# Fixing TensorE's order in the edge stage of a four-layer graph network

## The chip, the cores and the metric

The kernel runs on one core of a Trainium2 chip. The metric is the time of one execution on the device, in microseconds (us); lower is better. The times below are medians of several executions, and a profile is one further execution, with a time of its own.

## The reference

A graph of 3125 nodes and 103125 directed edges (50000 edges in both directions, and a loop at every node), sorted by destination, goes through four layers with a residual and a layer norm around each:

```python
x = _layernorm(x + _L0_gnn_ref(x, src, dst, edge_weight, L0_gnn_weight, L0_gnn_b))   # weighted sum over edges, relu
x = _layernorm(x + _L1_gnn_ref(x, edge_index, ...))                                  # attention, four heads
x = _layernorm(x + _L2_gnn_ref(x, L2_gnn_Wq, ..., edge_index))                       # attention, one head
x = _layernorm(x + _L3_gnn_ref(x, edge_index, ...))                                  # two mean aggregations
```

Layer 0 matters here: with `xw = x @ weight`, every edge adds its weight times `xw[dst]` to its source node's row; then bias and relu.

## The kernel before

The nodes are padded to 3200, 25 blocks of 128. Rather than gather and scatter edge by edge, the kernel turns the edge list into two dense 3200 x 3200 matrices in DRAM: counts of edges (`f_ctd`, bf16, used by layers 1 to 3) and sums of edge weights (`wd`, float32, used by layer 0). The stage that does it is the edge stage, inside `fast_path` (line 506 on).

**Batches and groups.** Five destination nodes make a window; there are 640 windows, in 40 batches of 16 (loop at line 852). A window has 256 slots for edges, in two halves of 128, one edge to a partition. For each slot the kernel makes two one-hot rows: `ohd` (the source's place in its block, 128 wide) and `ohc` (destination in the window and source block, 125 of 128 used). `make(b)` (line 811) does it for a whole batch on VectorE: `ohd` and `ohc` by comparing keys with a ramp (line 824), then `wod`, the one-hots of the source scaled by the weight in three bf16 parts (line 833). The second half of the third part is scaled by ScalarE, a window at a time, in `more(k)` (line 842). `make(b + 1)` is called as batch b begins.

Within a batch, four groups of four windows follow each other. A group is eight counting matmuls (line 864: out `cp`) and 24 weighted matmuls (line 872: out `wp`), each into a PSUM bank; ScalarE copies `cp` into `cs` (line 877) and `wp` into `ws` (line 883). After a batch, `ws` is stored to `wd` in two DMAs (line 885), and after every second batch `cs` is stored to `f_ctd` (line 888). All of these DMAs are issued by SyncE (SP), whose queue is taken in order.

**Keys.** The keys of a batch come from `keys_of(g)` (line 652), once for eight batches: three columns of a gathered table are copied out (VectorE and ScalarE), TensorE transposes them in six steps (lines 672 to 674), and VectorE and ScalarE make from these the bf16 pairs that `make` reads. For groups 2 to 4 the source calls `keys_of` in `make` at batches 10, 18 and 26 (one batch ahead, so while batches 9, 17 and 25 are traced).

**Layer 0 within the edge stage.** As soon as 128 further rows of `wd` are written, `add0` (line 784) loads them (the columns of the first 20 blocks, in two DMAs of 640 KB into tiles `cw`, line 790) and multiplies them by a block of `xw` in 20 float32 matmuls (line 794) that add to five PSUM banks, `acc0`. There are 25 such blocks of rows; those whose rows are not ready when the 40th batch ends follow after it. `end0` (line 799) then takes relu, residual and layer norm. The last five column blocks (`left`) are summed afterwards, in 25 more loads, while layer 1 begins.

**Buffers.** One-hots `ohd`, `ohc` have two buffers each (line 564), `wod` six, two batches' worth (line 565); PSUM tiles `cp` and `wp` share three banks (line 567); `cw` has three (line 806), so a load can run at most three tiles ahead of the products that read it; `cs` and `ws` have two (line 807).

**What sets the order.** The kernel is written for a tracing layer: the source says what depends on what, and a scheduler places each engine's instructions, taking those that it expects to be ready, by priority in the order of the source. It also adds all waits. So the source's order and the order on an engine are not the same: in the program before, the 20 matmuls of one `add0` stand together as one burst, in the midst of some group, and the bursts lie about one and a half batches apart. Once built, the order on each engine is fixed.

Of the kernel before, what the change touches and what calls it, by code (L numbers as in the profile page):

```python
# [8 lines left out]
BF16 = mybir.dt.bfloat16  # L9
# [6 lines left out]
P = 128  # L16
# [476 lines left out]
BW = 16  # L493
KW = WN * NB
NBT = NW // BW
Z0 = 20
# [9 lines left out]
def fast_path(  # L506
# [4 lines left out]
    nc = tc.nc  # L511
# [46 lines left out]
    xw = cst.tile([P, NB, P], F32, name="f_xw")  # L558
# [4 lines left out]
    kp = front.enter_context(tc.tile_pool(name="kp", bufs=2))  # L563
# [85 lines left out]
        )  # L649
        egs.append(eg)  # L650

    def keys_of(g):

        eg = egs[g]
        kd2 = kp.tile([P, P // BW, 2, BW, 2], BF16, name="kd2")
        kc2 = kp.tile([P, P // BW, 2, BW, 2], BF16, name="kc2")
        w2 = [kp.tile([P, P // BW, 2, BW, 2], BF16, name=f"w2_{s}") for s in range(3)]
        kic = ep.tile([P, EW], F32, name="kic", bufs=2)
        nc.vector.tensor_scalar(
            kic.rearrange("p (a k) -> p a k", k=16), eg[:, :, 0, :], thr[:, g : g + 1], None, OP.subtract  # L660
        )

        nc.vector.memset(kic[:, EW - 1 : EW], -1.0)
        kid = ep.tile([P, EW], F32, name="kid", bufs=2)
        nc.vector.tensor_copy(kid.rearrange("p (a k) -> p a k", k=16), eg[:, :, 1, :])
        wei = ep.tile([P, EW], F32, name="wei", bufs=2)
        nc.scalar.copy(wei.rearrange("p (a k) -> p a k", k=16), eg[:, :, 2, :])
        t0 = cps.tile([P, 4, P], F32, name="t0", tag="cw")
        t1 = cps.tile([P, 2, P], F32, name="t1", tag="cw")
        for h in range(2):  # L670
            a = slice(h * P, (h + 1) * P)
            nc.tensor.transpose(t0[:, h, :], kid[:, a], ident)
            nc.tensor.transpose(t0[:, 2 + h, :], kic[:, a], ident)
            nc.tensor.transpose(t1[:, h, :], wei[:, a], ident)

        def each(i, h):
            return i[:, h, :].rearrange("p (b w) -> p b w", w=BW)

        def pairs(i, h):
            return each(i, h)[:, :, :, None].to_broadcast([P, P // BW, BW, 2])  # L680

        wt = ep.tile([P, 2, P], F32, name="wt", bufs=2)
        wu = kp.tile([P, 2, P], F32, name="wu")
        for h in range(2):
            copy(kd2[:, :, h, :, :], pairs(t0, h))
            copy(kc2[:, :, h, :, :], pairs(t0[:, 2:, :], h))
            nc.scalar.copy(w2[0][:, :, h, :, :], pairs(t1, h))
        for s, (i, o) in enumerate(((t1, wt), (wt, wu))):
            for h in range(2):
                nc.vector.tensor_tensor(each(o, h), each(i, h), w2[s][:, :, h, :, 0], OP.subtract)  # L690
                nc.scalar.copy(w2[s + 1][:, :, h, :, :], pairs(o, h))
        return kd2, kc2, w2, wu

    keys = {0: keys_of(0), 1: keys_of(1)}


    l0_wt = load("f_l0_wt", l0_w, [P, P])
# [82 lines left out]
    def bias0(acc, n):  # L780
        for j in range(n):
            nc.tensor.matmul(acc[:, j, :], ones, l0_br, start=(j == 0), stop=False, skip_group_check=True)

    def add0(pool, i, accs, blocks):

        b0, n = blocks
        for h in range(0, n, 10):
            m = min(10, n - h)
            cw = pool.tile([P, min(10, n), P], F32, name="cw")[:, 0:m]
            nc.sync.dma_start(  # L790
                cw.rearrange("p c d -> p (c d)"), wd[i * P : (i + 1) * P, (b0 + h) * P : (b0 + h + m) * P]
            )
            for j in range(h, h + m):
                nc.tensor.matmul(  # L794
                    accs[j // 4][:, j % 4, :], cw[:, j - h, :], xw[:, i, :], start=False,
                    stop=(i == NB - 1 and (j % 4 == 3 or j == n - 1)), skip_group_check=True,
                )

    def end0(acc, b0, n):
        t = lp0.tile([P, 4, P], F32, name="r0")  # L800
# [5 lines left out]
    zp = front.enter_context(tc.tile_pool(name="f_zp", bufs=3))  # L806
# [3 lines left out]

    def make(b):

        if b % 8 == 2 and 8 < b < NBT - 8:
            keys[b // 8 + 1] = keys_of(b // 8 + 1)
        kd2, kc2, w2, w3 = keys[b // 8]
        ohd = op_.tile([P, 2 * BW, P], BF16, name="ohd")
        ohc = op_.tile([P, 2 * BW, P], BF16, name="ohc")

        def twos(k):
            k = k[:, b % 8, :, :, :].rearrange("p q w t -> p (q w) t")  # L820
            return k[:, :, None, :].to_broadcast([P, 2 * BW, P // 2, 2])

        for o, k in ((ohd, kd2), (ohc, kc2)):
            nc.vector.tensor_tensor(
                o.rearrange("p w (a t) -> p w a t", t=2), twos(k),
                ramp.rearrange("p (a t) -> p a t", t=2)[:, None, :, :].to_broadcast([P, 2 * BW, P // 2, 2]),
                OP.is_equal,
            )
        wod = []
        for s in range(3):  # L830
            f = of_.tile([P, 2 * BW, P], BF16, name="wod")
            n = 2 * BW if s < 2 else BW
            nc.vector.tensor_tensor(  # L833
                f[:, 0:n].rearrange("p w (a t) -> p w a t", t=2), ohd[:, 0:n].rearrange("p w (a t) -> p w a t", t=2),
                twos(w2[s])[:, 0:n], OP.mult,
            )
            wod.append(f)

        def more(k):
            for w in range(k, k + 4):  # L840
                at = (b % 8) * BW + w
                nc.scalar.activation(wod[2][:, BW + w, :], ohd[:, BW + w, :], AF.Copy, scale=w3[:, 1, at : at + 1])  # L842

        return ohd, ohc, wod, more

    cs = None
    acc0 = None
    done = 0
    cur = make(0)
    for k in range(0, BW, 4):  # L850
        cur[3](k)
    for b in range(NBT):
        ohd, ohc, wod, _ = cur
        cur = make(b + 1) if b + 1 < NBT else None
        if b % SB == 0:
            cs = sp.tile([P, NB, SB * BW * WN], BF16, name="cs")
        ws = sp.tile([P, BW, P], F32, name="ws")
        for k in range(0, BW, 4):
            cp = cps.tile([P, 4, P], F32, name="cp", tag="cw")
            wp = cps.tile([P, 4, P], F32, name="wp", tag="cw")  # L860
            for j in range(4):
                for q in range(2):
                    w = q * BW + k + j
                    nc.tensor.matmul(  # L864
                        cp[:, j, 0:KW], ohd[:, w, :], ohc[:, w, 0:KW], start=(j == 0 and q == 0), stop=(j == 3 and q == 1),
                        skip_group_check=True,
                    )
            for j in range(4):
                for q in range(2):
                    w = q * BW + k + j  # L870
                    for s in range(3):
                        nc.tensor.matmul(  # L872
                            wp[:, j, :], ohc[:, w, :], wod[s][:, w, :], start=(j == 0 and q == 0 and s == 0),
                            stop=(j == 3 and q == 1 and s == 2), skip_group_check=True,
                        )
            i0 = (b % SB) * BW * WN + k * WN
            nc.scalar.copy(  # L877
                cs[:, :, i0 : i0 + 4 * WN].rearrange("p c (w i) -> p c w i", i=WN),
                cp[:, :, 0:KW].rearrange("p w (i c) -> p c w i", c=NB),
            )  # L880
            if cur:
                cur[3](k)
            nc.scalar.copy(ws[:, k : k + 4, :], wp)  # L883
        for a, e in ((0, 112), (112, KW)):
            nc.sync.dma_start(wv_[b * BW : (b + 1) * BW, a:e, :].rearrange("w k d -> k w d"), ws[a:e, :, :])
        if b % SB == SB - 1:
            i0 = (b - SB + 1) * BW * WN
            nc.sync.dma_start(ctd[:, :, i0 : i0 + SB * BW * WN].rearrange("c d i -> d c i"), cs)
        if b < 2:
            for blocks in GB[4 * b : 4 * b + 4]:  # L890
                xw_of(*blocks)
        if b == 2:
            products_of_weights()
            acc0 = [zps.tile([P, 4, P], F32, name=f"acc{k}", tag=f"acc{k}") for k in range(Z0 // 4)]
            for a in acc0:
                bias0(a, 4)
        while acc0 and (done + 1) * P <= (b - 1) * BW * WN:
            add0(zp, done, acc0, (0, Z0))
            done += 1
    for i in range(done, NB):  # L900
        add0(zp, i, acc0, (0, Z0))
    front.close()
# [431 lines left out]
    with ExitStack() as st:  # L1334
# [79 lines left out]
        for x_, (q, c) in enumerate(items):  # L1414
# [6 lines left out]
            if q == 0 and NB - 4 <= c < NB - 1:  # L1421
                a = split + (c - NB + 4) * 512
# [6 lines left out]
            elif c == NB - 1:  # L1429
# [5 lines left out]
                for k0 in range(0, n, 3):  # L1435
# [5 lines left out]
                    for j in range(m):  # L1441
                        b = i0 + k0 + j
# [177 lines left out]
```

## Time and profile before

| | |
|---|---|
| median of 3 runs | 1538.35 us (1538.09 to 1540.38) |
| the profiled execution | 1536.56 us, span 1534.5 us |
| granted TensorE clock | 0.979 of full speed on average |
| TensorE, VectorE, ScalarE busy | 1400.5, 981.0, 923.4 us |
| first and last weighted matmul of the edge stage | 40.6 and 468.8 us after the span's start |
| last product into `acc0` | 497.9 us |

The span runs from the first to the last instruction; the time of the execution is 2.06 us longer. PE is TensorE's matmul, PEld its weight load, DVE is VectorE, ACT ScalarE, SP SyncE. A row of the timeline gives start and length of a run of equal instructions, and in brackets the idle time of the engine before it with what ended it. A matmul's end is modelled, so consecutive matmuls overlap in the records, and the distance from start to start is what one costs in a stream. A float32 product shows as two records.

### The profile page before, as it was taken

The numbers are of one execution on the slowest core, as the hardware profiler recorded it, in microseconds if no ns is written. First come the engines' busy times: TensorE is split into PE (matmuls) and PEld (weight loads), VectorE is DVE, ScalarE is ACT, GpSimd is POOL, SyncE is SP. The second block draws the span as 40 slices with busy tenths as digits, with TensorE's granted clock in tenths as the row PEclk, the third lists the DMA queues.
The fourth block names the chain that finished last, engine by engine and source line by source line (L and its number), as shares of the span: only waits on it lengthen the run. The fifth ranks groups of instructions, "written<-read, shape, count | busy, mean of one in ns | idle before, by whom it ended". The sixth has DMA issues, their size and how long they took to land.

```text
span 1534.5 us, 35155 instructions
## 1 busy us (share of the span) xinstructions
PE 1400.5 (91%) x14871; PEld 1223.6 (80%) x14871; DVE 981.0 (64%) x1574; ACT 923.4 (60%) x1880; POOL 122.5 (8%) x136
## 2 busy tenths in 40 slices
PE   4899999999997978899989989899999989999995
PEld 3898999998997867899979889577777764458995
DVE  4999899989991389778878887544464360012005
ACT  2988778888882489878778676544474340023006
POOL 1000000000000023203311320300000000000000
PEclk9999999999999999999999999999999999999998
DMA  6387787878877623444434333332222226513551
GB/s 192 91 220 207 203 234 206 235 202 223 214 214 232 222 85 101 143 118 125 132 115 134 114 87 95 106 94 68 67 72 73 82 105 238 193 44 129 195 195 45
DMA packets 210368, 224.39 MB, mean 146 GB/s; under 512 B 72892, under 2 KB 184007, under 8 KB 209945
## 3 DMA queue, kind: packets, MB, share of 16 engines
q1 hardware_dynamic: 206344, 217.74, 48.4%
q10 hardware_dynamic: 3457, 2.35, 0.6%
q8 instruction: 118, 1.93, 0.5%
q0 software_dynamic: 400, 1.97, 0.4%
q14 instruction: 49, 0.40, 0.1%
HBM read 157.67 MB, written 64.36 MB: 145 GB/s over the span
## 4 chain that ended last, share of the span: by engine, by line
PE 40%; DVE 5%; ACT 2%; issue 1%; POOL 1%; DMA 1%; DVEq 0%; ACTq 0%; SPq 0%; POOLq 0%
PE acc L1381 9%; PE s L1373 8%; PE acc L1476 7%; PE acc L1549 6%; PE acc L1241 4%; PE acc L1236 2%; DVE cm L1226 1%; DVE nz L1260 1%; PE tr L1513 1%; PE acc L1513 1%; DMA ct<-f_ctd 1%; ACT fm L1225 1%; DVE cm L1219 0%; PE tr L1505 0%; PE acc L1505 0%
## 5 line engine op out<-in xcount | busy, mean ns | idle before, releaser
L1241 PE MATMUL acc<-vp,cm 128*128 128x198 bf16 x2500 | 344.7, 252 | 6.6 <-DVE cm L1226 4.1
L1225 ACT ACTIVATE fm<-adr,bas 128x896 bf16<-128x896 f32 (+1 forms) x320 | 286.5, 952 | 68.0 <-DVE cm L1226 63.1
L1236 PE MATMUL acc<-vp,ct 128*128 128x204 bf16 x1250 | 315.2, 256 | 10.0 <-DVE vp L1144 5.6
L1241 PEld LDWEIGHTS <-cm 128*128 128x128 bf16 x2500 | 236.0, 98 | 26.5 <-issue 10.6
L872 PE MATMUL wp<-wod,ohc 128*128 128x128 bf16 x3840 | 244.0, 219 | 8.8 <-ACT cs L877 6.6
L872 PEld LDWEIGHTS <-ohc 128*128 128x128 bf16 x3840 | 224.0, 98 | 9.8 <-issue 9.4
L833 DVE TENSOR_TENSOR wod<-ohd,w 128x4096 bf16<-128x4096 bf16 (+1 forms) x120 | 225.0, 1931 | 0.6 <-PE wp L872 0.6
L1226 DVE TENSOR_TENSOR cm<-fm,ct 128x896 bf16<-128x896 bf16 (+1 forms) x320 | 198.1, 649 | 36.1 <-PE acc L1241 14.1
L842 ACT ACTIVATE wod<-ohd,wu 128x128 bf16<-128x128 bf16 x640 | 197.0, 400 | 0.0
L1377 DVE TENSOR_TENSOR e<-e,ct 128x416 f32<-128x416 f32 (+1 forms) x175 | 110.4, 636 | 108.2 <-ACT e L1376 102.6
L1376 ACT ACTIVATE e<-s,f_nm 128x416 f32<-128x416 f32 (+1 forms) x175 | 111.5, 642 | 99.4 <-PE s L1373 94.1
L1381 PEld LDWEIGHTS acc<-self__8127,e 128*128 128x128 f32 x1250 | 148.4, 193 | 21.5 <-issue 19.7
L1373 PE MATMUL s<-yT,f_xT 128*128 128x416 f32 (+1 forms) x350 | 145.8, 552 | 4.6 <-ACT rt L1356 4.0
L1381 PE MATMUL acc<-self__8127,e 128*128 128x129 f32 x1250 | 148.7, 276 | 0.6 <-DVE e L1377 0.6
L794 PE MATMUL acc<-f_xw,cw 128*128 128x128 f32 x1000 | 118.4, 278 | 7.4 <-DMA cw<-wd 7.4
L1236 PEld LDWEIGHTS <-ct 128*128 128x128 bf16 x1250 | 122.4, 98 | 2.5 <-issue 1.5
L883 ACT COPY ws<-wp 128x512 f32<-128x512 f32 x160 | 93.6, 585 | 49.8 <-PE wp L872 48.2
L794 PEld LDWEIGHTS acc<-f_xw,cw 128*128 128x128 f32 x1000 | 115.0, 194 | 7.6 <-DMA cw<-wd 7.6
L864 PE MATMUL cp<-ohc,ohd 128*128 128x125 bf16 x1280 | 96.7, 218 | 21.1 <-ACT ws L883 17.9
L1373 PEld LDWEIGHTS s<-yT,f_xT 128*128 128x128 f32 x350 | 62.2, 191 | 57.7 <-issue 40.6
L1476 PE MATMUL acc<-ct,ip 128*128 128x512 bf16 (+1 forms) x525 | 104.9, 360 | 1.4 <-DMA ct<-f_ctd 1.4
L1549 PE MATMUL acc<-ip,ct 128*128 128x128 bf16 x1875 | 105.2, 219 | 0.0
(277 smaller groups left out, 1482.7 us busy)
## 6 DMA issues: line engine op xcount, KB each, us to landing
ct<-f_ctd SPq DMA_DIRECT2D x50, 800.0 KB
wd<-ws SPq DMA_DIRECT2D x40, 896.0 KB
ct<-f_ctd SPq DMA_DIRECT2D x150, 224.0 KB
cw<-wd SPq DMA_DIRECT2D x50, 640.0 KB
f_ctd<-cs SPq DMA_DIRECT2D x20, 1000.0 KB
ct<-f_ctd SPq DMA_DIRECT2D x25, 416.0 KB
ct<-f_ctd SPq DMA_DIRECT2D x25, 384.0 KB
cw<-wd SPq DMA_DIRECT2D x25, 320.0 KB
```

The costliest lines, as they stand in the source:

```text
L794: nc.tensor.matmul(accs[j // 4][:, j % 4, :], cw[:, j - h, :], xw[:, i, :], start=False, stop=(i == NB - 1 and (j % 4 == 3 or j == n - 1)) ...
L833: nc.vector.tensor_tensor(f[:, 0:n].rearrange("p w (a t) -> p w a t", t=2), ohd[:, 0:n].rearrange("p w (a t) -> p w a t", t=2), twos(w2[s] ...
L842: nc.scalar.activation(wod[2][:, BW + w, :], ohd[:, BW + w, :], AF.Copy, scale=w3[:, 1, at : at + 1])
L872: nc.tensor.matmul(wp[:, j, :], ohc[:, w, :], wod[s][:, w, :], start=(j == 0 and q == 0 and s == 0), stop=(j == 3 and q == 1 and s == 2), ...
L1225: nc.scalar.activation(f[:, : n * P], at, AF.Relu, bias=bas[:, c, h : h + 1], scale=UP)
L1226: nc.vector.tensor_tensor(m[:, : n * P], f[:, : n * P], ct[:, : n * P], OP.min)
L1236: nc.tensor.matmul(out_(F1, PW), ct[:, k * P : (k + 1) * P], vp[:, c, hp : hp + 2, :, 2 * F1 : V1], start=(c == 0), stop=False, skip_group ...
L1241: nc.tensor.matmul(out_(0, 2 * F1)[:, j], ms[j][:, k * P : (k + 1) * P], vp[:, c, hp + j, :, 0 : 2 * F1], start=False, stop=(c == NB - 1 a ...
L1373: nc.tensor.matmul(s[:, :m], xT[:, c * P : (c + 1) * P], yT[:, i0 * P + a : i0 * P + a + m], start=True, stop=True)
L1381: nc.tensor.matmul(acc[k // 3][:, (k % 3) * (P + 1) : (k % 3 + 1) * (P + 1)], es[q, c][:, k * P : (k + 1) * P], vo[:, c, 0 : P + 1], start ...
L1476: nc.tensor.matmul(acc[k][:, :n], ips[b // 4][:, b % 4, s, :], ct[:, c : c + n], start=(b == 0 and s == 0), stop=(b == NB - 1 and s == 2),)
L1549: nc.tensor.matmul(acc[g][:, j, :], ct[:, (b0 + j) * P : (b0 + j + 1) * P], ups[b // 4][:, b % 4, s, :], start=(b == 0 and s == 0 and j == ...
```

## The change

Three things are changed, all in the edge stage. First, `add0` is divided: `adds0` issues the loads and returns the 20 matmuls as a list of functions; the loop puts them on a list, `todo`, and takes four from it behind each group. Second, after batch 2 (counted from 0) a context is entered in which the scheduler keeps the order of the source on TensorE alone; it is left when the last batch and the rest of `todo` are traced. The other engines are scheduled as before. Third, `keys_of` is divided: `columns_of` copies the columns out, called in `make` at batches 9, 17 and 25, and the transposes and all behind them are called at batches 11, 19 and 27.

```diff
-    def keys_of(g):
+    def columns_of(g):
         eg = egs[g]
...
         nc.scalar.copy(wei.rearrange("p (a k) -> p a k", k=16), eg[:, :, 2, :])
+        return kid, kic, wei
+
+    def keys_of(kid, kic, wei):
...
-    keys = {0: keys_of(0), 1: keys_of(1)}
+    keys = {g: keys_of(*columns_of(g)) for g in range(2)}
...
-    def add0(pool, i, accs, blocks):
+    def adds0(pool, i, accs, blocks):
         b0, n = blocks
+        todo = []
...
             for j in range(h, h + m):
-                nc.tensor.matmul(
-                    accs[j // 4][:, j % 4, :], cw[:, j - h, :], xw[:, i, :], start=False,
+                todo.append(lambda j=j, a=cw[:, j - h, :]: nc.tensor.matmul(
+                    accs[j // 4][:, j % 4, :], a, xw[:, i, :], start=False,
                     stop=(i == NB - 1 and (j % 4 == 3 or j == n - 1)), skip_group_check=True,
-                )
+                ))
+        return todo
+
+    def add0(*args):
+        for f in adds0(*args):
+            f()
...
     def make(b):
-        if b % 8 == 2 and 8 < b < NBT - 8:
-            keys[b // 8 + 1] = keys_of(b // 8 + 1)
+        if b % 8 == 1 and 8 < b < NBT - 8:
+            keys[b // 8 + 1] = columns_of(b // 8 + 1)
+        if b % 8 == 3 and 8 < b < NBT - 8:
+            keys[b // 8 + 1] = keys_of(*keys[b // 8 + 1])
...
             nc.scalar.copy(ws[:, k : k + 4, :], wp)
+            for f in todo[:4]:
+                f()
+            del todo[:4]
...
             for a in acc0:
                 bias0(a, 4)
+
+            order = ExitStack()
+            order.enter_context(tc.manual_schedule(engines={mybir.EngineType.PE}))
         while acc0 and (done + 1) * P <= (b - 1) * BW * WN:
-            add0(zp, done, acc0, (0, Z0))
+            todo += adds0(zp, done, acc0, (0, Z0))
             done += 1
+    for f in todo:
+        f()
+    order.close()
     for i in range(done, NB):
         add0(zp, i, acc0, (0, Z0))
```

More of the change, by code (lines that the diff above doesn't have):

```diff
@@ L650, in fast_path @@
         egs.append(eg)
-    def keys_of(g):
+    def columns_of(g):
         eg = egs[g]
-        kd2 = kp.tile([P, P // BW, 2, BW, 2], BF16, name="kd2")
-        kc2 = kp.tile([P, P // BW, 2, BW, 2], BF16, name="kc2")
-        w2 = [kp.tile([P, P // BW, 2, BW, 2], BF16, name=f"w2_{s}") for s in range(3)]
         kic = ep.tile([P, EW], F32, name="kic", bufs=2)
@@ L667, in keys_of @@
         nc.scalar.copy(wei.rearrange("p (a k) -> p a k", k=16), eg[:, :, 2, :])
+        return kid, kic, wei
+    def keys_of(kid, kic, wei):
+        kd2 = kp.tile([P, P // BW, 2, BW, 2], BF16, name="kd2")
+        kc2 = kp.tile([P, P // BW, 2, BW, 2], BF16, name="kc2")
+        w2 = [kp.tile([P, P // BW, 2, BW, 2], BF16, name=f"w2_{s}") for s in range(3)]
         t0 = cps.tile([P, 4, P], F32, name="t0", tag="cw")
@@ L848, in fast_path @@
     done = 0
+    todo = []
+    order = None
     cur = make(0)
```

## The prediction

> **What bounds the kernel now.** The page first: TensorE is the busiest engine, and the change concerns the first twelve of its forty slices, where VectorE is as full.
>
> ```profile
> span 1534.5 us, 35155 instructions
> PE 1400.5 (91%) x14871; PEld 1223.6 (80%) x14871; DVE 981.0 (64%) x1574; ACT 923.4 (60%) x1880; POOL 122.5 (8%) x136
> PE   4899999999997978899989989899999989999995
> DVE  4999899989991389778878887544464360012005
> ```
>
> Next the busy times by stretch (span, PE, PEld, DVE, ACT, POOL, then clock and DMA): eight batches of the edge stage, then the wait between the last batch and layer 0's last product.
>
> ```profile
> 178.60:266.70 88.10, 81.97 (x1230) 80.64 (x1230) 80.62 (x47) 71.53 (x198) 0.00 (x0) 1.00 0.79 213
> 468.80:497.90 29.10, 21.06 (x170) 20.60 (x170) 3.68 (x23) 2.31 (x4) 1.45 (x2) 0.88 0.75 221
> ```
>
> Eight batches take 88.1 us with PE and DVE both near 81: neither is fed all the time. The table of waits from 82.8 to 460 us says why (total, times, longest):
>
> ```profile
> DVE ohd L824 <- PE cp L864: 21.1, 16, 1.7
> PE cp L864 <- ACT ws L883: 17.9, 15, 1.6
> PE wp L872 <- ACT cs L877: 4.2, 5, 1.3
> ```
>
> DVE can't start a batch's one-hots until PE has read those of two batches before; PE waits for ACT to empty PSUM. Prices come from the PE timeline:
>
> ```profile
> 220.33 0.60 PE L864 MATMUL cp<-ohc,ohd 128*128 128x125 bf16 x8
> 220.77 1.50 PE L872 MATMUL wp<-wod,ohc 128*128 128x128 bf16 x24
> 222.11 0.60 PE L864 MATMUL cp<-ohc,ohd 128*128 128x125 bf16 x8
> 237.50 4.68 PE L794 MATMUL acc<-f_xw,cw 128*128 128x128 f32 x40
> 242.02 0.44 PE L864 MATMUL cp<-ohc,ohd 128*128 128x125 bf16 x5
> ```
>
> From start to start a group is 222.11 - 220.33 = 1.78 us, a batch of four 7.1. A product is two records, so twenty take 242.02 - 237.50 = 4.52, four 0.90. Eight batches hold 32 groups (56.8), 100 products (22.6) and six key transposes (0.8): 80.2 of PE. The other 8 are waits, mostly 1.6 us ones behind batches without products, where PE outruns ACT. DVE needs 9.95 a batch (2.2 + 2.2 + 5.55) and 1.6 for keys: 81.2. So a perfect order could win 7 us in eight batches.
>
> Loads come through SP's queue behind the stores:
>
> ```profile
> 224.70 2.01 SPq L885 DMA_DIRECT2D wd<-ws  x2
> 226.81 2.80 SPq L790 DMA_DIRECT2D cw<-wd  x2
> ```
>
> The trace's single packets (5120 bytes in a load, 512 in a store) show this first load complete at 233.1: 8.4 us after its store was issued; 8.1 to 8.7 in the like cases. No product in the stage waits today: loads are complete 1.4 to 5.2 us before their first product. The one wait is after the last batch, and a slow clock follows it:
>
> ```profile
> 487.28 5.90 PE L794 MATMUL acc<-f_xw,cw 128*128 128x128 f32 x38 [7.37 <-DMA cw<-wd]
> 483.40:490.20 6.80, 2.92 (x13) 2.92 (x14) 0.06 (x1) 0.00 (x0) 0.00 (x0) 0.50 0.92 317
> ```
>
> [...] Here a product whose load is late therefore holds every group behind it. [...] a load's own packets take 2 to 4.8 us but end 8.4 after the store ahead. [...] here 7.37 us of idleness gave 6.8 us at 0.50, and gaps of 2.3 to 2.4 us at 551 and 575 us gave 3.4 us at 0.50 each.
>
> **The change part by part.** No arithmetic is added or removed; the built program of the changed kernel shows the new order. Name W, S the stores of a batch (weights; counts, after odd batches) and L0, L1, ... the loads, two to each twenty products.
>
> *Products spread.* Bursts of 4.5 us become pieces of 0.9. Switching costs nothing (starts stay 0.055 and 0.11 us apart across a switch). A group with products takes PE 2.68; ACT needs 0.59 + 0.59 + 1.27 = 2.45, so there PE stops outrunning ACT. Seven of 32 groups have none; following ACT's new order through three PSUM buffers I get waits of 0.5 (after batch 16), 0.3 (19) and 1.5 (21): 2.3 in eight batches.
>
> *Keys in two steps.* Columns are ready a batch or two earlier, so PE's transposes, now fixed at the end of batches 9, 17, 25, wait for nothing. DVE's 1.6 us are as before. ACT now does all four casts of w before a group's weights leave PSUM: PE waits 1.0 three groups on (0.77 and 0.50 in the present one).
>
> *PE keeps the source's order.* This is the dear part. Of SP's order the pieces that matter are: S5 W5 L3 before batch 6, W14 L14 L15 L16 before 15, and the same at L24, L34, L44. PE wants L14 after the second group of batch 15, while W14 leaves only after batch 14's last products were copied. From the end of those: copy 1.2 (ACT has four scalings ahead of it, 1.27), store to load complete 8.4, semaphore 0.8 (from the packets' end at 486.5 to PE at 487.28): ready at +10.4. PE arrives at +5.2 (products 0.9, group, products, group, less 0.2 for the pipeline's end): a stall of 5.2. DVE can't cover it: its next one-hots wait for the last counts of batch 15. By the clock rows above the stall brings one slow window, part of it hidden in the stall; with its phase unknown the loss is 0.4 to 1.7, taken 1.1. L19, behind S17 and W17, is ready at +13.3 (12.6 in the like case of batch 19, plus semaphore) and wanted at 12.9: 0.4; L39, without keys before it, 2.0.
>
> Eight batches: 80.2 + 5.2 + 1.1 + 2.3 + 1.0 + 0.4 = 90.2, against 88.2.
>
> *The sum, in us of the profiled execution.* Batch 6 starts its groups at 103.2. L3, behind S5 (103.9 as before) and W5, is complete near 116 (now 116.9), so PE, arriving at 110.7, stalls to some 116.6; with six products, a group and 1.1 of slow clock batch 6 ends at 120.8. Batches 7 to 13: 28 groups 49.7, 84 products 19.0, transposes 0.8, waits 1.0 + 0.4 + 2.4 = 73.3, so batch 14 starts at 194.1 (now 191.4, with as many products done). Three cycles, the last without keys and with 2.0 at L39: 90.2 + 90.2 + 90.0, to 464.5 (now 449.3, twenty products behind: 4.5 us of work). Batch 38's weights end at 474.5; L44 is ready at 484.9, two groups, eight products and 1.1 of slow clock end the stage at 491.4 (now 468.6). After it 52 products remain instead of 80, bound by the loads as now: L47 behind S39 and W39 ready at 12.6 + 0.7, ten products at half clock 3.9 (487.3 to 491.2 now), twenty more 4.4: 21.6 against 29.3. Layer 0's first accumulation ends at 513.0 instead of 497.9, 15 us late. Behind it the program is the same, and TensorE is busy for 46.2 of the next 47.4 us, so this moves to the end one for one: 1536.6 + 15 = 1551.6. The runs' median lies 1.8 above the profiled execution: 1553.
>
> Bounds: the stall can't fall below 2.0 (copy 0.6, store issued 2.1, load issue to complete 4.4 at the least), nor pass 6.5 (store to complete 9.5); five of them span 23 us. Waits on ACT are 0 to 4 in eight batches, on keys 0 to 1.5.
>
> **Rivals.**
> 1. *Faster: loads are in time.* Place: L14 and its like. For it: SP is idle for some 8 us ahead of W14, and today no product waits. Against: the store is ahead of the load in its queue. If each load were complete when PE comes, the cycle is 80.2 + 3.7 = 83.9, 4.3 better, the batches before 14 gain 7 on my sum, and the end loses 6.3 of stall: 15 - 7 - 3 x 6.3 - 2 - 6.3 = -19, so 1519. It decides below 2.8 us a stall, slow clock included: the five cost 7 + 4 x 6.3 = 32 in my sum, and 15 + 3 of it must go.
> 2. *Stalls as forecast, but ACT keeps up everywhere.* For it: ACT's 2.45 fits into a group with products, and a stall lets it catch up. Against: seven groups in 32 have none. 2.4 fewer before batch 14 and 2.3 in each cycle, 9.3 in all: 1544.
> 3. *Milder stalls:* no slow clock [...] and loads 1.5 us earlier (no queue ahead of W14): 5 x 2.6 = 13 off: 1540, no change.
> 4. *The loads' queue backs up*, since DMA is 0.79 busy already: each stall 1.5 longer: 1561.
> That the change isn't made is excluded by the built order.
>
> **How the numbers follow.** My forecast 0.50, rival 1 0.14, rival 2 0.16, rival 3 0.12, rival 4 0.08. About 0.2% (3.1 us) is what a measurement can tell from no change: below 1535.3 are rival 1 and a quarter of rival 3, 0.17; from there to 1541.4 the rest of rival 3 and the low end of rival 2, 0.12; above, 0.71. The forecast's own range is 1545 to 1559. From 1537 to 1562 leaves out rival 1, part of rival 3 and the end of rival 4.
>
> **What would show it.** Right: PE rows of products with gaps of about 5 us until the load, in batches 6, 15, 23, 31, 39; slow clock after them; DVE's wait for PE near or above 21 us in fewer, longer pieces; the last group near 491; fewer products behind it. Wrong: no wait of products in the stage; waits on ACT above 10 us in eight batches; an end of the stage before 470.

## The result, and the profile after

The changed kernel takes 1548.01 us, median of 6 runs (1545.33 to 1553.08), against 1538.14 for the kernel before in the same comparison: a ratio of 1.0068 with a 95% interval of 1.0054 to 1.0082, so about 10 us slower. The profiled execution took 1548.64 us, its span 1546.6 (12.1 more than before). The page's first lines:

```profile
span 1546.6 us, 35165 instructions
PE 1410.9 (91%) x14871; PEld 1234.9 (80%) x14871; DVE 980.9 (63%) x1574; ACT 924.7 (60%) x1880; POOL 122.9 (8%) x136
```

PE has the same 14871 matmul records and is busy 10.4 us longer: that is the first hint of a slower clock, since no work was added. The waits of PE and of VectorE inside the stage, from 82.8 us to 484.5 (total, times, longest):

```profile
DVE ohd L836 <- PE cp L878: 31.7, 8, 8.4
...
PE acc L799 <- DMA cw<-wd: 24.6, 6, 5.4
...
PE wp L886 <- ACT cs L891: 2.8, 3, 0.9
...
PE cp L878 <- ACT ws L897: 1.9, 6, 0.4
```

Products now wait for loads, which never happened in the stage before; the waits on ACT are down from 22.1 us to 4.7; VectorE's waits for PE came together from 16 pieces of at most 1.7 us into 8 of up to 8.4. One of the stalls, as PE's timeline has it, and under it SP's timeline of the same moment:

```profile
207.78 0.60 PE L878 MATMUL cp<-ohc,ohd 128*128 128x125 bf16 x8
208.22 1.50 PE L886 MATMUL wp<-wod,ohc 128*128 128x128 bf16 x24
214.31 2.08 PE L799 MATMUL acc<-f_xw,cw 128*128 128x128 f32 x8 [4.59 <-DMA cw<-wd]
216.18 1.05 PE L878 MATMUL cp<-ohc,ohd 128*128 128x125 bf16 x8
217.02 2.53 PE L886 MATMUL wp<-wod,ohc 128*128 128x128 bf16 x24
```

```profile
205.21 1.98 SPq L902 DMA_DIRECT2D wd<-ws  x2
207.28 3.76 SPq L795 DMA_DIRECT2D cw<-wd  x3
```

This is batch 15 behind its second group: L14 leaves only after W14, 7 us before its first product runs. After the stall the same eight counts take 1.05 us instead of 0.60 and the weights 2.53 instead of 1.50. There are five windows with half the granted clock inside the stage, at 116.8, 212.3, 304.5, 393.2 and 482.0 us; by stretch (columns as in the tables before), two of them and the sum of all five:

```profile
212.30:219.10 6.80, 4.79 (x36) 4.73 (x37) 0.80 (x1) 2.43 (x8) 0.00 (x0) 0.50 0.56 219
304.50:307.90 3.40, 3.29 (x22) 3.23 (x23) 0.00 (x0) 0.37 (x2) 0.00 (x0) 0.50 0.59 240
...
sum 27.20, PE 21.40 PEld 21.10 DVE 1.83 ACT 5.65 POOL 0.00; mean PE 4.28 PEld 4.22 DVE 0.37 ACT 1.13 POOL 0.00
```

PE worked 21.4 us in them, at half speed: 10.7 us lost. The stage before had no such window.

Layer 0's last product of the first accumulation comes 15.9 us late (513.8 against 497.9). What the tables show of it: waits on loads +24.6, slow clock in the stage +10.7, all waits of PE on ACT and VectorE -18.7 (23.9 to 5.2), the wait behind the last group -1.0 (7.4 to 6.4), in sum +15.6. That this comes so close is chance, since the tables leave out two things of like size and opposite sign. The first is a price of the spreading:

```profile
201.38 1.11 PE L799 MATMUL acc<-f_xw,cw 128*128 128x128 f32 x8
202.32 0.60 PE L878 MATMUL cp<-ohc,ohd 128*128 128x125 bf16 x8
```

A piece of four products takes 0.94 us from start to start, where its eight records at 0.112 us would take 0.90: behind a switch from bf16, the second record starts 0.165 us after the first. Between 82.8 us and the stage's end there are 107 such switches instead of 22, 4.5 us more. The second is the part of PE's waits that a modelled end covers, so that the tables don't count it: a bf16 matmul is shown as 0.22 us long, though in a stream the next starts after 0.056. From start to start, the waits on ACT and VectorE fell by about 25 us instead of 18.7.

Behind that point the trace gives 3.8 us back. The same 47.4 us, before and after:

```profile
497.90:545.30 47.40, 46.24 (x338) 40.05 (x339) 19.75 (x77) 20.94 (x47) 4.82 (x16) 0.93 0.61 197
```

```profile
513.80:561.20 47.40, 44.78 (x352) 39.00 (x351) 22.58 (x85) 23.19 (x50) 5.18 (x18) 1.00 0.65 206
```

Both kernels have a slow window behind the last wait, ahead of this stretch (483.4 to 490.2 before, 502.5 to 509.3 after). The kernel before has a second one at 500.5 to 507.3, inside the stretch (clock 0.93), which costs it half of 6.8 us; after the change there is none (clock 1.00), and 14 more matmuls fit.

### The profile page after: what moved, and what is told of

It is laid out like the page before. It is cut to its first block, busy times and chain, and to the rows that moved or that the text cites. A ratio compares the mean times of both kernels' runs of the same rounds, so it can differ in the third digit from the quotient of the medians.

```text
span 1546.6 us, 35165 instructions
## 1 busy us (share of the span) xinstructions
PE 1410.9 (91%) x14871; PEld 1234.9 (80%) x14871; DVE 980.9 (63%) x1574; ACT 924.7 (60%) x1880; POOL 122.9 (8%) x136
## 3 DMA queue, kind: packets, MB, share of 16 engines
q0 software_dynamic: 400, 1.97, 0.4%
## 5 line engine op out<-in xcount | busy, mean ns | idle before, releaser
L854 ACT ACTIVATE wod<-ohd,wu 128x128 bf16<-128x128 bf16 x640 | 201.0, 396 | 0.4 <-DVE ohd L836 0.2
L799 PE MATMUL acc<-f_xw,cw 128*128 128x128 f32 x1000 | 143.8, 290 | 31.0 <-DMA cw<-wd 31.0
L799 PEld LDWEIGHTS acc<-f_xw,cw 128*128 128x128 f32 x1000 | 126.9, 200 | 32.2 <-DMA cw<-wd 32.2
L891 ACT CAST cs<-cp 128x500 bf16<-128x500 f32 x160 | 92.4, 578 | 57.7 <-PE cp L878 57.5
L836 DVE TENSOR_TENSOR ohd<-kd,ramp 128x4096 bf16<-128x4096 bf16 x40 | 91.6, 2290 | 34.0 <-PE cp L878 31.7
```

The source lines that it names most:

```text
L799: todo.append(lambda j=j, a=cw[:, j - h, :]: nc.tensor.matmul(accs[j // 4][:, j % 4, :], a, xw[:, i, :], start=False, stop=(i == NB - 1 an ...
```

## The experiments

The theory under test is the prediction's: late loads, held in order by TensorE, and slow clock behind them. Each ratio is to the kernel before, run beside it on the same chip, where it took 1535.3 to 1538.1 us; differences between runs below are by the ratios. All of them together, by what they combine ("two-step" and "one-step" are the keys; products spread four at a time, or in bursts of twenty):

| loads' queue | TensorE's order | products, keys | run | us | ratio, 95% |
|---|---|---|---|---|---|
| SP | scheduler's | bursts, one-step | before | 1538.1 | 1 |
| SP | scheduler's | bursts, two-step | keys_alone | 1541.3 | 1.0035 (1.0022 to 1.0047) |
| SP | scheduler's | spread, two-step | free_order | 1540.8 | 1.0039 (1.0025 to 1.0053) |
| SP | source | bursts, two-step | bursts | 1575.5 | 1.0259 (1.0242 to 1.0277) |
| SP | source | spread, two-step | the change | 1548.0 | 1.0068 (1.0054 to 1.0082) |
| SP | source | spread, one-step | change_keys_one_step | 1554.9 | 1.0118 (1.0098 to 1.0137) |
| SP, loads ahead of stores | source | spread, two-step | ahead | 1526.2 | 0.9937 (0.9920 to 0.9953) |
| SP | source | spread a batch later, two-step | lag | 1528.0 | 0.9947 (0.9930 to 0.9964) |
| GpSimd | scheduler's | bursts, one-step | before_poolq | 1538.8 | 1.0014 (1.0001 to 1.0026) |
| GpSimd | source | bursts, two-step | bursts_poolq | 1523.3 | 0.9916 (0.9900 to 0.9933) |
| GpSimd | source | spread, two-step | poolq | 1514.5 | 0.9863 (0.9843 to 0.9883) |
| GpSimd | source | spread, one-step | poolq_keys_one_step | 1520.5 | 0.9894 (0.9878 to 0.9911) |
| GpSimd | scheduler's | spread, two-step | poolq_free_order | 1515.1 | 0.9867 (0.9851 to 0.9884) |
| GpSimd | source | spread a batch later, two-step | poolq_lag | 1517.0 | 0.9882 (0.9866 to 0.9899) |

### Are the late loads the cause, and what makes them late?

Three ways to have a load in time: want it later, issue it ahead of the store, give it a queue without stores.

**lag**

```diff
+        todo += fresh
+        fresh = []
         while acc0 and (done + 1) * P <= (b - 1) * BW * WN:
-            todo += adds0(zp, done, acc0, (0, Z0))
+            fresh += adds0(zp, done, acc0, (0, Z0))
             done += 1
-    for f in todo:
+    for f in todo + fresh:
```

> The changed kernel with one thing moved: products become due one batch later (a batch's loads go through a list called fresh before their products are handed out); the loads keep their place behind the stores on SP's queue. Theory (late loads): the load that arrives 10 us after its batch's end is now wanted about 17 us after it, so the five stalls of 4.5 to 5.4 us (23.8 us in the trace of the changed kernel) and the slow clock behind them (an estimate: 10 us) go, and waits on ACT grow by some 5; no PE wait of a product on a load inside the stage above 0.5 us; a cycle of eight batches 82 to 84 us instead of 90.3. Time 1517 (1509 to 1525), below both kernels. Rival (the fixed order itself costs PE's slack): the 5 us gaps turn into waits of the groups on ACT and DVE, a cycle stays near 88 to 90 and the time at 1540 to 1548.

Measured: 1528.0, faster than both kernels, and 3 us above the expected range. There is no slow window in the stage, and L14 and its like no longer stall. But cycles of eight batches take 86.8, 86.3 and 83.9 us, because other loads are now the late ones. The first row of PE's waits in the stage up to 460 us, then one of them on PE's timeline, and SP's timeline ahead of it:

```profile
PE acc L799 <- DMA cw<-wd: 6.9, 5, 2.3
```

```profile
268.68 1.16 PE L799 MATMUL acc<-f_xw,cw 128*128 128x128 f32 x8 [2.26 <-DMA cw<-wd]
```

```profile
255.57 6.05 SPq L903 DMA_DIRECT2D wd<-ws  x2
261.71 2.60 SPq L795 DMA_DIRECT2D cw<-wd  x2
```

That product is L20's, and L20 stands on SP's queue behind S19 and W19, with which SP is occupied until 261.6. L30 and L40 are alike (1.7 and 1.8 us). The expectation had followed only L14 and its like through the new order; every load has to be followed.

**ahead**: the block that issues loads, moved.

```diff
+        while acc0 and (done + 1) * P <= (b - 1) * BW * WN:
+            todo += adds0(zp, done, acc0, (0, Z0))
+            done += 1
         for a, e in ((0, 112), (112, KW)):
             nc.sync.dma_start(wv_[b * BW : (b + 1) * BW, a:e, :].rearrange("w k d -> k w d"), ws[a:e, :, :])
...
-        while acc0 and (done + 1) * P <= (b - 1) * BW * WN:
-            todo += adds0(zp, done, acc0, (0, Z0))
-            done += 1
```

> The changed kernel with the block that issues loads moved in the source from behind a batch's stores to ahead of them; TensorE's order in the stage is the same, products are due as before. On SP's queue L14, L15 now stand ahead of W14 (and L4, L24, L34, L44 ahead of their stores), while L6, L16, L26, L36 stand behind the counts and weights of a batch (S15 W15 L16). Theory (late because the store is ahead in the queue, not because of the data): no stall at L14 and its like; a smaller one at L6, L16, L26, L36: ready about 13 us after the last group of the batch, wanted 10.7 after it, 2 to 3 us each, four times. Time 1528 (1518 to 1536). Rival (the load waits for its data, the store of the batch just ended): the stalls stay at about 5 us and the time at 1545 or above.

Measured: 1526.2. The stalls at L14 and its like are gone; L6, L16, L26, L36, now the ones behind a batch's stores, stall 2.0, 1.3, 1.6 and 2.0 us, somewhat less than expected, and two slow windows of 3.4 us are left in the stage. L16's on PE's timeline:

```profile
223.96 1.16 PE L799 MATMUL acc<-f_xw,cw 128*128 128x128 f32 x8 [1.29 <-DMA cw<-wd]
```

TensorE's order in the stage is the changed kernel's, so 20 us came from the order on SP's queue alone. The data were there: L14 holds rows 896 to 1023, and with 80 rows a batch W12 is the last store that it needs.

**poolq**

```diff
-            nc.sync.dma_start(
+            nc.gpsimd.dma_start(
                 cw.rearrange("p c d -> p (c d)"), wd[i * P : (i + 1) * P, (b0 + h) * P : (b0 + h + m) * P]
             )
```

> The changed kernel with layer 0's loads issued by GpSimd instead of SyncE, so on a queue without stores; TensorE's order in the stage is the same. Each load waits by semaphore for the stores of its own rows and for its buffer. Theory (queue order): L14 needs rows stored a batch and a half earlier, so it goes as soon as L11's buffer is read, and no product stalls in the stage; a cycle of eight batches 82 to 84 us, time 1516 (1508 to 1524). Rival (three cw buffers are too few, or the rows are not there): a load is issued no earlier than now, stalls of 4 to 6 us stay, time 1540 to 1555.

Measured: 1514.5, 1.4% below the kernel before. The first fence is GpSimd's timeline where L14 leaves, the second PE's at L14's first product, the third the two largest of PE's waits in the stage up to 450 us, the fourth the eight batches 14 to 21 by stretch:

```profile
192.86 0.53 POOL L795 DMA_DIRECT2D cw<-wd  x1 [10.59 <-DMA wd<-ws]
```

```profile
205.08 1.11 PE L799 MATMUL acc<-f_xw,cw 128*128 128x128 f32 x8
```

```profile
PE cp L878 <- ACT ws L897: 4.3, 9, 1.6
PE wp L886 <- ACT cs L891: 2.6, 3, 0.9
```

```profile
189.50:273.20 83.70, 82.02 (x1230) 81.20 (x1230) 81.52 (x47) 71.96 (x202) 5.28 (x10) 1.00 0.86 228
```

L14 leaves as W12 has landed, 12 us before its product and ahead of the end of batch 14 (199.8); the product's row has no bracket. No wait on a load is left in the stage and no slow clock. PE and VectorE are both busy for over 97% of the cycle. With three buffers as before, the rival that they are too few is out.

### What the order and the spreading do

**bursts**

```diff
-            for f in todo[:4]:
-                f()
-            del todo[:4]
...
-            todo += adds0(zp, done, acc0, (0, Z0))
+            add0(zp, done, acc0, (0, Z0))
             done += 1
-    for f in todo:
-        f()
     order.close()
```

> The changed kernel without the spreading: TensorE keeps the order of the source, but the twenty products of a block of rows follow directly where their loads stand in the source, behind the last group of a batch. In the built program L15 stands behind W14 on SP's queue (so do L5, L25, L35, L45), and its products directly behind the last group of batch 14. Theory (a product held in order behind a store and a load): ready about 11 us after that group, wanted 2.2 after it, so a stall of 8 to 9 us five times, with slow clock behind each: a cycle of 92 to 96 us, time 1570 (1558 to 1585), slower than the changed kernel. Rival (spreading is what costs, because it delays products): stalls go, time 1535 to 1542 as before the change.

Measured: 1575.5. A product wanted sooner waits longer: PE's waits on loads in the stage, and one of its slow windows (34 us of them in the stage):

```profile
PE acc L799 <- DMA cw<-wd: 39.4, 21, 5.5
```

```profile
213.10:223.30 10.20, 7.73 (x34) 7.43 (x35) 6.07 (x4) 3.15 (x11) 0.00 (x0) 0.50 0.90 269
```

The sum is close to the expected five times 8 to 9 us, its pieces are not: 21 waits of up to 5.5 us, L14 and L15 sharing one delay. Spreading therefore softened the fixed order; it did not cause the loss.

**bursts_poolq**: the same edit, with the loads on GpSimd's queue.

> The changed kernel with the products in bursts of twenty behind a batch's last group (not spread), TensorE in source order, and the loads issued by GpSimd. Against the run with spreading on GpSimd's queue it differs only in the spreading; against the run with bursts on SP's queue only in the queue. Theory: no product stalls on a load (a block of rows is stored a batch or more before its burst), so the 1575 of the bursts on SP's queue falls by the stalls, some 34 us, and their slow clock; but a burst of 4.5 us lets ACT run dry and a batch without products is followed by PE waits on ACT: a cycle of 86 to 89 us, time 1533 (1525 to 1541). Rival (spreading is worth nothing, only the order counts): cycle 83 to 84, 1517 or less.

Measured: 1523.3, a little below the theory's range and above the rival's. The stalls are gone, as they should be. Of the waits on ACT that the theory had laid to bursts, PE's table up to 460 us keeps little:

```profile
PE cp L878 <- ACT ws L897: 0.3, 2, 0.2
```

The same row has 17.9 us in the kernel before. But most of these waits have only become too short for the table. Three rows of PE's timeline in batch 16, which follows a batch without products, and between them one of ACT's:

```profile
210.43 0.60 PE L878 MATMUL cp<-ohc,ohd 128*128 128x125 bf16 x8
210.91 1.50 PE L886 MATMUL wp<-wod,ohc 128*128 128x128 bf16 x24
211.91 0.59 ACT L897 COPY ws<-wp 128x512 f32<-128x512 f32 x1
212.55 0.60 PE L878 MATMUL cp<-ohc,ohd 128*128 128x125 bf16 x8
```

The group takes 2.12 us from start to start instead of 1.78, without a bracket, and the next one starts as ACT's copy ends (212.50). Counted in this way over batches 14 to 21, PE's waits cost about 5.5 us here, 8.1 in the kernel before and 2.1 in poolq. So waits on ACT remain, as the theory has it, but they are fewer than it took. In source order a burst stands at a batch's end; the scheduler of the kernel before had put bursts into the middle of a batch. That this made the waits shorter is argued, not shown. The first two cycles take 85.6 us, 2 more than spread. Spreading by itself is worth 8 us (0.9916 against 0.9863), although its switches cost about 1 us in eight batches.

**before_poolq**: the kernel before with the GpSimd edit alone.

> The kernel before with one thing changed: layer 0's loads are issued by GpSimd instead of SyncE. Theory (the gain of the run with GpSimd's queue comes from spreading the products and the order, once the loads are in time): the kernel before had no product waiting for a load inside the stage, so only small things move: bursts of 4.5 us and PE's waits on ACT stay, a cycle of eight batches 86 to 89 us, time 1533 (1526 to 1540). Rival (the queue alone is the gain, since SP's stores and the loads hinder each other): 1520 or less.

Measured: 1538.8, inside the range but for another reason: the first two cycles take 92 us (the third 83), and

```profile
PE acc L794 <- DMA cw<-wd: 20.1, 3, 7.0
```

is the only row in PE's table of waits in the stage. With the loads on another queue the scheduler itself pulled the first products of L8, L18 and L28 up between counts and weights of a batch's first group, where the loads come 6 to 7 us late; a slow window of 6.8 us follows each. So the queue alone gains nothing, but this run can't say what the kernel before would gain from it with products in their old places.

**poolq_free_order** and **free_order** leave the fixed order out, on GpSimd's and on SP's queue:

```diff
-            order = ExitStack()
-            order.enter_context(tc.manual_schedule(engines={mybir.EngineType.PE}))
...
-    order.close()
```

> The run with GpSimd's queue, without the fixed order: TensorE's order is the scheduler's own. With the loads off SP's queue the scheduler itself leaves the products four at a time nearly where the source has them (a few are one matmul block earlier, the transposes at the end of the same batches). Theory (the fixed order in itself is worth nothing when loads are in time): 1515 (1511 to 1519), no difference from the run with fixed order. Rival (fixed order is a gain of its own): 1522 or more.

> The changed kernel without the fixed order: products handed out four at a time in the source and keys in two steps, loads on SP's queue, TensorE's order left to the scheduler. In the built program it puts most products in bursts of 20 one to four groups later than the source, L14's behind the second group of batch 16 instead of batch 15. Theory (the fixed order is what makes the late loads cost): no product waits on a load inside the stage above 0.5 us, a cycle of 86 to 89 us, 1535 (1529 to 1540). Rival (the stalls come with the spreading of the source, whoever sets the order): 1543 or more.

Measured: 1515.1 and 1540.8. With the loads on GpSimd's queue the fixed order gains nothing (0.9867 against 0.9863). The two are equal in sum, not in their waits: PE's table of waits up to 456 us has one row in poolq_free_order,

```profile
PE acc L799 <- DMA cw<-wd: 6.7, 3, 2.7
```

where poolq has 7.4 us of waits on ACT and VectorE and none on loads. The scheduler had put some products where their loads come up to 2.7 us late, and a slow window of 3.4 us begins at the first of these, at 101.4 us. On SP's queue a free order avoids all five stalls: PE's list of waits has no load in it. It is then 4 us faster than the change (1.0039 against 1.0068), still slower than before and just above the expected range. The likely reason is in the keys.

### The keys

**keys_alone**: the kernel before with `columns_of` at `b % 8 == 1` and `keys_of` at `b % 8 == 3`, as in the change. Products come in bursts through `add0`, but `add0` is divided too, so in the source both loads of a block stand ahead of its twenty products instead of one ahead of each ten.

> The kernel before with the keys' two steps alone: products in bursts where the scheduler puts them, loads on SP's queue, no fixed order. Theory: with a free order the scheduler had already moved the transposes to where they wait little; the columns' 1.6 us of VectorE stay the same. A saving of at most 1 us for each of three keys: 1534 (1530 to 1538), no difference from before that could be told. Rival (the second step is a gain of 2 us each as on GpSimd's queue): 1530 or less.

Measured: 1541.3, 5.4 us slower than before by the ratio; neither theory said so. PE's waits in the stage add up to what they were (23.8 against 23.9 us). What differs is PE's timeline where the transposes now stand:

```profile
142.99 0.33 PE L676 MATMUL t<-f_ident,kid 128*128 128x128 f32 x1 [1.57 <-ACT ws L897]
...
145.10 1.00 PE L878 MATMUL cp<-ohc,ohd 128*128 128x125 bf16 x8 [1.21 <-ACT ws L897]
146.76 1.97 PE L886 MATMUL wp<-wod,ohc 128*128 128x128 bf16 x17 [0.66 <-ACT cs L891]
```

and the clock behind them, by stretch, the first of three windows and the sum:

```profile
144.40:151.20 6.80, 5.44 (x38) 5.28 (x38) 6.76 (x9) 5.58 (x18) 0.00 (x0) 0.50 0.79 196
...
sum 17.00, PE 14.97 PEld 14.65 DVE 16.87 ACT 12.84 POOL 0.00; mean PE 4.99 PEld 4.88 DVE 5.62 ACT 4.28 POOL 0.00
```

The transposes fall into the wait behind a batch without products, ahead of two more waits: 3.4 us of idleness within 5.3, in three pieces. The clock fell at 144.4 us, before the last of them was over. A slow window comes at each of the three keys, here and in free_order, and PE works 15 us in these at half speed, 7.5 lost. In the kernel before the same waits lie further apart, and it has no slow window in the stage. That the packing of the waits slows the clock is argued from these six places; no run changed it alone. In keys_alone the scheduler also put some bursts a little earlier or later, and no run has free_order's edits with keys in one step.

**poolq_keys_one_step** and **change_keys_one_step**: one step again, under the fixed order.

```diff
-        if b % 8 == 1 and 8 < b < NBT - 8:
-            keys[b // 8 + 1] = columns_of(b // 8 + 1)
-        if b % 8 == 3 and 8 < b < NBT - 8:
-            keys[b // 8 + 1] = keys_of(*keys[b // 8 + 1])
+        if b % 8 == 2 and 8 < b < NBT - 8:
+            keys[b // 8 + 1] = keys_of(*columns_of(b // 8 + 1))
```

> The run with GpSimd's queue, with keys prepared in one step again, at batches 10, 18, 26 as before the change. Theory (the second step matters once TensorE's order is fixed): PE's six transposes stand at the end of batches 8, 16, 24 and wait there for VectorE's columns, and VectorE waits for the transposes: 1 to 1.5 us each of three times, 1518 (1515 to 1522). Rival (hidden by slack): 1514.5 as with two steps, within 0.1%.

> The changed kernel with keys prepared in one step, at batches 10, 18, 26 as before: spreading, fixed order and SP's queue stay. TensorE's transposes then stand at the end of batches 8, 16, 24. Theory (the second step pays under a fixed order, here as on GpSimd's queue, where undoing it cost 6 us): the five stalls on loads stay at 4.5 to 5.4 us and the keys cost 1.5 to 2 us more each of three times: 1553 (1549 to 1557). Rival (in the free order the two steps alone cost 5.5 us, so they cost here too): 1543 or less.

Measured: 1520.5 and 1554.9, 5 and 8 us above the same kernels with two steps (0.9894 against 0.9863, 1.0118 against 1.0068). So the two steps cost 5 us under the scheduler's order, with bursts, and save 5 to 8 under a fixed one, with products spread. In the second kernel the stalls on loads stay as they were (25.3 us in 6), and slow windows in the stage grow from 27.2 to 34 us. Three of them, of 3.4 us each, begin soon behind the transposes (at 144.4, 236.6 and 328.7 us); PE is busy for 10.1 us in these at half speed, so about 5 of the 8 us are lost there.

### One step further

**poolq_lag**: the edits of lag and poolq together.

> The run with GpSimd's queue, and products due one batch later as in the lag run. Theory (what kept the lag run at 1528 was L20, L30, L40 behind W19, W29, W39 on SP's queue, not the three cw buffers): no stall above 0.5 us in the stage, its end some 2 us earlier than with GpSimd's queue alone because 12 more products stand behind the last group, where they fill the wait for the last load: 1513 (1509 to 1516). Rival (a buffer is read a batch later, so three are too few): stalls of 2 us at several loads, 1520 or more.

Measured: 1517.0, between the two. PE's list of waits in the stage has no load, so what kept lag back was SP's queue and not three buffers. Its first row is now

```profile
PE cp L879 <- ACT ws L898: 6.9, 12, 1.6
```

But PE waits more for ACT (6.9 against 4.3), the first two cycles take 84.8 and 84.4 (83.7 and 83.3 in poolq; the third is alike), and the twelve products kept for the end save nothing: the stage ends at 459.3 (459.2 in poolq) and the first accumulation 1.2 us later. By the intervals this is no difference that can be told from poolq. poolq and poolq_free_order have the lowest times, 2% below the changed kernel and 1.4% below the one before.

## Why the prediction was right

The forecast was 1553; 1548.0 lies in its own range, and the step that decides, late loads held in order, is shown. That the number came so close is in part luck: four terms were off, and their errors cancel. By its steps:

- *Stalls.* All five came where forecast, in batches 6, 15, 23, 31 and 39: 5.4, 4.6, 4.5, 4.6 and 4.7 us for 5.2. The runs lag, ahead and poolq, each of which takes the lateness away by another means, turn the loss into a gain. L39's 2.0 was 0.8, L19's 0.4 didn't show. In all 24.6 us of waits on loads, against 29.9 by the forecast's terms (5.9, four times 5.2, three times 0.4, and 2.0).
- *Slow clock* was taken at 1.1 us a stall and is 2.1: 10.7 us in the stage for 5.5. The choice of one window of 3.4 us each, partly hidden, was too mild; three of the five brought 6.8. The windows began 0.1 to 2.4 us before the late product started.
- *Waits on ACT.* With the keys' 1.0 each, 12.3 us were forecast for the stage; PE waited 5.2 for ACT and VectorE together, 2.8 of it at the keys, 0.9 each as forecast. The step that failed is the rest: following ACT's order through three PSUM buffers by hand gave 2.3 a cycle, 9.3 in all, and 2.4 were measured. At most a part of that is stalls that let ACT catch up, for in poolq, without stalls, all these waits are 7.4. Rival 2 had this term nearly right.
- *PE's work.* "Switching costs nothing" was wrong. The starts on either side of a switch are as close as was read, but the second record of each piece comes 0.053 us late, 102 times from batch 6 to the stage's end: 5.4 us, of which the price taken from a burst held only 1.1. From batch 6's start at 103.2 the stage lasts 389.0 us (388.2 forecast). Without the three terms above, that leaves about 8 us more for PE's work than the forecast's sum; besides the switches these are parts of waits that modelled ends cover.
- *The sum.* Cycles of 90.4, 89.6 and 90.1 us (90.2, 90.2, 90.0), the stage's end at 492.2 (491.4), the first accumulation at 513.8 (513.0). It held because loads (-5.3) and waits on ACT (-7.1) came out lower, the clock (+5.2) and PE's work (+8) higher.
- *"Moves to the end one for one"* failed: 15.9 us became 12.1. PE's busy time behind the stage looked like work, but part of it was work at half clock, and that window did not move along. The median was also taken 1.8 above the profiled execution, as in the kernel before; it is 0.6 below. These two make up the difference of 5 us to the forecast.
- *Rival 1* was wrong of the changed kernel, but its working for loads in time, 1519, is close to what poolq measured. Rivals 3 and 4 had the stalls too small and too large.
- *Keys* were taken as free of cost but for 1.0 of ACT (0.9 measured). In the fixed order they even save; the prediction's sum did not separate that.

## What to carry to other kernels

TensorE, with its order fixed by hand, stood still for 4.5 to 5.4 us at five products whose loads were late, so before fixing an order, follow every load through the built order of its queue: here a load stood behind a store that it did not need, and a queue of its own turned +0.7% into -1.4%. With that in place the order needed no fixing at all; without it, the scheduler's own order was hiding the lateness. Parts of a change don't add up when each shifts the others' waits: the keys' two steps cost 5 us beside bursts in the scheduler's order and save 5 to 8 beside spread products in a fixed one, so try each part beside the others, not only by itself. And a table of waits isn't the whole loss: measure a stream from start to start, where short waits and the price of a switch show.

## What the runs showed of the hardware

**The clock.** Each of the changed kernel's five stalls of 4.5 to 5.4 us brought 3.4 or 6.8 us at half clock. The five falls in its stage (116.8, 212.3, 304.5, 393.2 and 482.0 us) lie 95.5, 92.2, 88.7 and 88.8 us apart, which is 28, 27, 26 and 26 times 3.41, and the slow windows read in this case's stages last 3.4, 6.8 or (in bursts) 10.2 us. In the 3.41 us ahead of each of the five falls PE was idle for 2.2 to 3.4. By stretch of 3.41 us, first ahead, where a product waited 1.97 us for its load, then lag with its wait of 2.26 us, and last the stretch ahead of the first fall in keys_alone (after the times: length, PE's busy time; the third number from the end is the clock):

```profile
135.61:139.02 3.41, 1.46 (x17) 1.45 (x18) 3.41 (x2) 3.41 (x12) 0.00 (x0) 1.00 0.99 341
139.02:142.43 3.41, 3.41 (x31) 3.41 (x29) 3.41 (x3) 3.31 (x10) 0.00 (x0) 0.50 1.07 311
```

```profile
264.42:267.83 3.41, 2.00 (x36) 1.82 (x33) 3.41 (x3) 3.41 (x10) 0.00 (x0) 1.00 0.86 260
267.83:271.24 3.41, 2.56 (x37) 2.55 (x38) 3.41 (x3) 3.41 (x13) 0.00 (x0) 1.00 1.09 353
```

```profile
141.02:144.43 3.41, 1.30 (x14) 0.91 (x12) 3.41 (x3) 3.41 (x11) 0.00 (x0) 1.00 0.81 285
```

The shorter wait lay within one stretch, which was idle for 1.95 us, and the clock was at half in the next; the longer one was split over two (1.4 and 0.85 us), and the clock stayed at 1.00 in both. In keys_alone no single wait of PE in the stage was above 1.6 us, but the 3.41 us ahead of its first two falls were idle for 2.1 and 1.9. So the length of a single wait did not tell in these runs whether the clock fell. Nor is there a length of idleness to carry elsewhere: behind the stage of the kernel before, the clock was at half from 500.5 us on, after 3.41 us with 1.18 idle (from 497.1), and stayed at 1.00 after 3.41 us with 1.70 idle (from 589.2). What sets a fall is not shown.

**Two queues.** GpSimd issued a load in 0.53 us. In poolq the DMA share of a cycle rose from 0.80 (191.6 to 279.8 us in the kernel before) to 0.86; the same bytes in 83.7 instead of 88.2 us account for 0.84. A new row of waits appeared on ACT, whose copies of weights wait for earlier stores to land (up to 500 us); whether loads on the other queue slow these stores is not shown:

```profile
ACT ws L897 <- DMA wd<-ws: 15.8, 8, 5.4
```

PE, busy for 98% of the cycle, lost little by it.
